# Places for other steps among the scans of a vision network: products at a unit's end, readings at the next one's beginning

## The chip, the cores and the metric

The kernel runs on one core of a Trainium2 chip. A core has five engines, each with its own queue of instructions that it takes strictly in order: TensorE (PE, matrix products, which reach their readers only through the small memory PSUM), VectorE (DVE), ScalarE (ACT), GpSimd (POOL), and SyncE (SP), which issues most transfers. Engines wait for one another by semaphores. The metric is the device time of one execution in microseconds (us); less is better.

## The reference

A two-layer network on four images of 256 channels and 32x32 pixels (1024 pixels an image), all in float32. Layer 0 (an attention with a selection of scores, and a mixture of eight small experts) is not touched by the change. Layer 1 is

```python
x = x + L1_conv(ln_c(x))                    # selective scan in four directions
t = tokens(x); x = x + L1_ffn(ln_t(t))      # two of eight experts for each token
```

with the two parts cut to what matters:

```python
def _selective_scan(x, A_log, D, W_delta, b_delta, W_B, W_C):
    delta = softplus(x @ W_delta + b_delta)
    Bm, Cm = x @ W_B, x @ W_C               # 16 states
    dA = exp(delta[..., None] * -exp(A_log))
    dBx = (delta * x)[..., None] * Bm[:, :, None, :]
    h = scan of  h = dA * h_before + dBx  over the 1024 pixels
    return einsum('bln,blcn->blc', Cm, h) + x * D
# the mean of four scans: forward, backward, rows from the last, columns from the last

def _L1_ffn(x, Wr, br, ln_g, ln_b, W1, b1, W2, b2):
    top_p, top_idx = top_k(softmax(x @ Wr + br), 2)
    xn = (x - mean) * rsqrt(var + 1e-5)
    y[e] = gelu((xn * ln_g[e] + ln_b[e]) @ W1[e] + b1[e]) @ W2[e] + b2[e]   # 256 -> 1024 -> 256
    return the two chosen y, weighted by top_p / sum(top_p)
```

## The kernel before, in words

**Scans.** An image is kept with channels on partitions, as two halves `c` of 128 channels. The kernel goes through 4 images x 2 halves x 16 states = 128 *units*, written out by hand under a manual schedule: the function `turn(k)` issues the instructions in the order in which each engine will take them. Per unit VectorE runs three scans of 128x1024: `forth` (L1505) over the pixels, `back` (L1514) over them backwards, and `columns` (L1531); and the small scan `come` (L1520). The third direction comes from the forward scan by a correction that GpSimd multiplies out (`third`, L1525). TensorE adds the four directions in PSUM by products with an identity matrix (`add`, L1500; `columns`, L1535), into two PSUM tiles `hp` per unit. VectorE multiplies them with C (`output`, `yc`, L1541), and TensorE sums the 16 states into `y` (L1542). After 16 states VectorE adds `y` to `x` (L1545). ScalarE makes the decays (`da_c` L1479, `prod` L1483, `da` L1487) and turns the inputs to columns (`uu` L1493), one unit ahead; GpSimd makes `uu` (L1492). At the first state of a half VectorE makes the running sum `cum` (L1571).

In `turn(k)` the order is: loads for unit k+2; `cum` and the column decays of k+1; `third` of k-1; products of k+1; `forth` and `back` of k; decays and inputs of k+1; `output` of k-1; `come_in` of k; then a place for *steps*; then `columns` of k.

**Steps.** Beside the scans other work goes in small pieces, written as generators that `yield` after each: `norm` (mean, transposes with the router's logits, variance, two reciprocal roots) and `route` (best two experts, ranks, slots) of the image whose scans have just ended, and `Prep.steps` of the next one: mean (`ln_mean` L1390), variance (`ln_var` L1399), scaling (`ln_rb`), B and C (`bp` L1426), and softplus in four blocks (`zp` L1438, ScalarE L1443 to L1449, VectorE L1447 to L1456, where `up` is L1447). The two are chained, first norm and route, then the preparation. Each unit takes one step, every fourth two, all in the place after `come_in`. A step often holds the reading of the previous step's product together with the next product. The steps' PSUM tiles share four buffers, tag `hp`, with the scans' own. After routing, `scatter` issues one indirect transfer a unit on GpSimd that puts tokens into their experts' slots.

**Experts.** The second stage goes over tiles of 256 tokens, each of one expert: `inputs` (transposes L1649, scaling to `xe` L1652, places of the results `to` L1655), `hidden` (L1664, Gelu on ScalarE L1666), `result` (L1672, `ys` L1675, and two indirect transfers L1677 on GpSimd to the rows that `to` names). 17 *early* tiles, of tokens of the first three images, run under a manual schedule with the steps of the last image's norm, route and scatter, one step after `hidden` and one after `result`. Then 19 *late* tiles follow. The tiles' buffers rotate in twos. A last stage adds each token's two results.

Of the kernel before, what the change touches and what calls it, by code (L numbers as in the profile page):

```python
# [11 lines left out]
F32 = mybir.dt.float32  # L12
F16 = mybir.dt.float16
BF16 = mybir.dt.bfloat16
I32 = mybir.dt.int32
# [6 lines left out]
P = 128  # L22
# [21 lines left out]
EARLY = (2 * (B - 1) * L - E * (T - 1) + T - 1) // T  # L44
W = C + 2
# [12 lines left out]
def metaformer(ctx: ExitStack, tc: tile.TileContext, t: dict, out: bass.AP):  # L58
# [1129 lines left out]
    def route(b, space, psum, tag):  # L1188

        used = 0  # L1190

        def room(shape):
            nonlocal used
            size = math.prod(shape)
            view = space[:, used : used + size]
            used += size
            return view if len(shape) == 1 else view.rearrange("p (a b) -> p a b", b=shape[1])
# [14 lines left out]
        best(m1, hot1)  # L1212
        nc.vector.tensor_scalar(tok[:, :, C + 1], red, -1.0, float(E), ALU.mult, ALU.add)
        nc.vector.tensor_copy(tok[:, :, C], goal[:, ts(b, NT)])
        yield
# [13 lines left out]
        nc.tensor.matmul(sums[:, 1].rearrange("p n e -> p (n e)"), mean_w, flat, start=True, stop=True)  # L1229
        nc.vector.tensor_scalar(m1, m2, 1.0, None, ALU.add)  # L1230
# [5 lines left out]
        place, pick, slotf = room([E, NT]), room([NT, E]), room([NT])  # L1236
        nc.vector.tensor_scalar(tote, sums[:, 1].rearrange("p n e -> p e n"), float(C), None, ALU.mult)
        nc.vector.tensor_copy(place, sums[:, 0].rearrange("p n e -> p e n"))
# [7 lines left out]
        yield  # L1246
        for k in range(2):
            nc.vector.tensor_tensor(pick, hots[k], place.rearrange("p e n -> p n e"), ALU.mult)
            nc.vector.tensor_reduce(slotf, pick, AX.X, ALU.add)
            nc.vector.tensor_copy(slot[:, k], slotf)  # L1250
        if b < B - 2:
            return
        yield
# [3 lines left out]
        if b == B - 2:  # L1257

            nc.vector.tensor_tensor(more, counts, limits, ALU.is_ge)
            nc.vector.tensor_reduce(tiles, more, AX.X, ALU.add)  # L1260
            ends = early.fill(room, tiles, done)
            nc.vector.tensor_tensor(left, tiles, ends, ALU.subtract)
            nc.vector.tensor_scalar(left, left, float(EARLY), 0.0, ALU.add, ALU.max)
            nc.vector.tensor_tensor(done[:, :E], left, tiles, ALU.min)
        else:

            nc.vector.tensor_scalar(count, count, float(T - 1), None, ALU.add)
            nc.vector.tensor_tensor(more, counts, limits, ALU.is_ge)
            nc.vector.tensor_reduce(tiles, more, AX.X, ALU.add)
            nc.vector.tensor_tensor(tiles, tiles, done[:, :E], ALU.subtract)  # L1270
            ends = late.fill(room, tiles, done)
            nc.vector.tensor_scalar(extra, ends[0:1, E - 1 : E], USUAL - EARLY + 0.5, None, ALU.is_gt)

# [9 lines left out]
    def norm(b, pool, psum, tag, raw_tag, d):  # L1283


        for h in range(NHALF):
            cols = ts(h, HALF)
            mean = psum.tile([P, HALF], F32, tag=tag, name="nm_mean")
            for c in range(CT):
                nc.tensor.matmul(mean, mean_w, x[b][:, c, cols], start=(c == 0), stop=(c == CT - 1))  # L1290
            yield
            for c in range(CT):
                nc.vector.tensor_tensor(d[:, c, cols], x[b][:, c, cols], mean, ALU.subtract)
        var = pool.tile([P, NT], F32, tag="nm_var", name="nm_var")
        raw = psum.tile([P, HALF], F32, tag=raw_tag, name="raw")[:, : NT * E].rearrange("p (n e) -> p n e", e=E)
        for r in range(NT // 2):
            tp = psum.tile([P, 2, C], F32, tag=tag, name="nm_tp")
            for i in range(2):
                n = 2 * r + i
                for c in range(CT):  # L1300
                    nc.tensor.transpose(tp[:, i, ts(c, P)], d[:, c, ts(n, P)], ident)
                for c in range(CT):
                    nc.tensor.matmul(raw[:, n], d[:, c, ts(n, P)], rw1[:, c, :], start=(c == 0), stop=(c == CT - 1))
            yield
            nc.scalar.copy(tok[:, ts(r, 2), :C], tp)
            for i in range(2):
                n = 2 * r + i
                nc.scalar.activation(tp[:, i], tp[:, i], AF.Square, scale=C ** -0.5, accum_out=var[:, n : n + 1])
        yield
# [3 lines left out]
        def rsqrt(dst):  # L1313

            nc.scalar.activation(sd, ve, AF.Sqrt)
            yield
            nc.vector.reciprocal(r0, sd)
            nc.vector.tensor_tensor(sd, r0, r0, ALU.mult)
            nc.vector.tensor_tensor(sd, sd, ve, ALU.mult)
            nc.vector.tensor_scalar(sd, sd, -0.5, 1.5, ALU.mult, ALU.add)  # L1320
            nc.vector.tensor_tensor(dst, r0, sd, ALU.mult)


        nc.vector.tensor_scalar(ve, var, 1e-5, None, ALU.add)
# [4 lines left out]
        nc.vector.tensor_tensor(lg1, raw, s1.unsqueeze(2).to_broadcast([P, NT, E]), ALU.mult)  # L1329
# [7 lines left out]
    with ExitStack() as st:  # L1337
# [34 lines left out]
        class Prep:  # L1372
# [9 lines left out]
            def steps(self):  # L1382
# [12 lines left out]
                yield  # L1395
                var = ps_m.tile([P, HALF], F32, tag="hp", name="ln_var")[:, :NT]
                for n in range(NT):
                    for c in range(CT):
                        nc.tensor.matmul(var[:, n : n + 1], sq[:, c, ts(n, P)], mean_w[:, 0:1],  # L1399
                                         start=(c == 0), stop=(c == CT - 1))  # L1400
                yield
                ve, sd, r0, rr, rs = (p1.tile([P, NT], F32, tag=f"ln_{i}", name=f"ln_{i}")
                                      for i in ("ve", "sd", "r0", "rr", "rs"))
                nc.vector.tensor_scalar(ve, var, 1e-6, None, ALU.add)
                nc.scalar.activation(sd, ve, AF.Sqrt)
                yield
# [4 lines left out]
                nc.vector.tensor_tensor(rs, r0, rr, ALU.mult)  # L1411
                for h in range(NHALF):
# [8 lines left out]
                yield  # L1421
                bc = p1.tile([P, 4 * HALF], F32, tag="sp", name="bc")[: 2 * NS, :L]
                for h in range(NHALF):
                    bp = ps_m.tile([P, HALF], F32, tag="hp", name="bp")[: 2 * NS]
                    for k in range(CT):
                        nc.tensor.matmul(bp, wbc[:, k, :], xm[:, k, ts(h, HALF)],  # L1426
                                         start=(k == 0), stop=(k == CT - 1))
                    nc.scalar.copy(bc[:, ts(h, HALF)], bp)
                nc.sync.dma_start(self.bc, bc)
                yield  # L1430


                for c in range(CT):
                    for h in range(NHALF):
                        cols = ts(h, HALF)
                        zp = ps_m.tile([P, HALF], F32, tag="hp", name="zp")
                        for k in range(CT):
                            nc.tensor.matmul(zp, wd[:, k, ts(c, P)], xm[:, k, cols],  # L1438
                                             start=(k == 0), stop=(k == CT - 1))
                        dd = self.delta[:, c, cols]  # L1440
# [4 lines left out]
                        nc.scalar.activation(v, v, AF.Exp, scale=-1.0)  # L1445
                        yield
# [4 lines left out]
                        yield  # L1451
                        nc.vector.tensor_tensor(v, v, ru, ALU.mult)
                        nc.vector.tensor_tensor(v, v, ln, ALU.add)
                        nc.vector.tensor_tensor(dd, dd, v, ALU.add)
                        nc.vector.tensor_tensor(self.dx[:, c, cols], dd, xm[:, c, cols], ALU.mult)  # L1455
                        nc.vector.scalar_tensor_tensor(x[b][:, c, cols], xm[:, c, cols], dsk[:, c : c + 1],  # L1456
                                                       x[b][:, c, cols], ALU.mult, ALU.add)
                    yield

        class Scan:  # L1460
# [51 lines left out]
            def back(self):  # L1512
                hs = p2.tile([P, L], F32, tag="h", name="h", bufs=4)
# [15 lines left out]
            def columns(self):  # L1529
                hs = p2.tile([P, L], F32, tag="h", name="h", bufs=4)  # L1530
# [20 lines left out]
        scans, steps, ys, cum = [], iter(()), [], None  # L1551
        sending = iter(())

        def routed(b):
            nonlocal sending
            yield from norm(b, p1, ps_m, "hp", "hp", p1.tile([P, CT, L], F32, tag="xm", name="nm_d"))
            yield from route(b, p1.tile([P, 4 * HALF], F32, tag="sp", name="numbers"), ps_m, "hp")
            sending = scatter(b)

        def turn(k):  # L1560
            nonlocal steps, cum
            if 0 <= k + 2 < len(order):
# [14 lines left out]
            if 0 <= k < len(order):  # L1577
                b, c, s = order[k]
                if c == 0 and s == 0:
                    for steps_left in (steps, sending):  # L1580
                        assert next(steps_left, "end") == "end"
                    steps = routed(b - 1) if b > 0 else iter(())
                    if b + 1 < B:
                        preps.append(Prep(b + 1))
                        steps = chain(steps, preps[-1].steps())
# [9 lines left out]
            if 0 <= k < len(order):  # L1595
                scans[k].come_in()
                for _ in range(1 + (s % 4 == 3)):
                    next(steps, None)
# [11 lines left out]
    with ExitStack() as st:  # L1610
# [3 lines left out]
        class Tile:  # L1614
# [28 lines left out]
            def inputs(self, ps_t):  # L1643
# [10 lines left out]
                self.to = pb.tile([P, T // P], I32, tag="to", name="to")  # L1654
# [13 lines left out]
            def result(self, ps_y):  # L1668
# [5 lines left out]
                ys = pb.tile([P, T // P, C], F32, tag="ys", name="ys")  # L1674
# [6 lines left out]
        with ExitStack() as sa:  # L1681
# [5 lines left out]
            with tc.manual_schedule():  # L1687
                todo = [Tile(early, i, "xa", EARLY) for i in range(EARLY)]
                for i in range(EARLY):
                    todo[i].slots()  # L1690
                    if i < 2:
                        todo[i].weights()
                b = B - 1
                steps = chain(norm(b, pa, psa, "t", "raw", pa.tile([P, CT, L], F32, tag="nm_d", name="nm_d")),
                              route(b, pa.tile([P, 4 * HALF], F32, tag="sp", name="numbers"), psa, "t"), scatter(b))
                next(steps)
                todo[0].inputs(ps_t)
                for i in range(EARLY):
                    todo[i].hidden(ps_h)
                    next(steps, None)  # L1700
# [5 lines left out]
                    next(steps, None)  # L1706
                for _ in steps:
                    pass
# [112 lines left out]
```

## Time and profile before

| | us |
|---|---|
| median of 3 runs | 4604.15 (4597.9 to 4604.52) |
| the profiled execution | 4614.54 |
| its span, first to last instruction | 4612.8 |
| scans, 128 units (2553.78 to 3897.50) | 1343.7 |
| early experts (to 4255.16) | 357.7 |
| late experts (to 4562.95) | 307.8 |
| last stage | 49.9 |

The first 2553.8 us are layer 0 and the preparation of image 0. In the profile, a line of the timeline gives start, duration, engine, source line, operation, the tiles written and read, their shapes, and in brackets how long the engine had stood idle before it and what ended that. A line of the waits gives who waited, for whom, the total in us, how often, and the longest. Consecutive equal instructions are merged (x4); matmuls are pipelined, so a group's start-to-start distance says more than its duration. Units are counted from 0, and unit k starts at the k-th `forth` scan.

### The profile page before, as it was taken

To read this page: it belongs to the slowest core of one execution; us is meant where nothing else is said; L and a number is where in the kernel's file an instruction comes from. 1 tells how busy PE (TensorE), PEld (TensorE's weight loads), DVE (VectorE), ACT (ScalarE), POOL (GpSimd) and SP (SyncE) were. 2 spreads that over 40 slices of the span, in tenths; PEclk is the share of its full clock that TensorE was granted. 3 is DMA by queue.
4 is the path that set the end of the run, shared out by engine and by line. 5 is a ranking of instruction groups with operands and counts; after the bars stand their busy time and mean duration, and the time that the engine had idled before them with its cause. 6 is when DMAs were issued, how large, how long until landed. Compare 5 with 4: busy or idle time off the path is not lost. (4 is left out here: it accounts for less than half of the span.)

```text
span 4612.8 us, 51296 instructions
## 1 busy us (share of the span) xinstructions
PE 3950.6 (86%) x18522; PEld 2185.2 (47%) x18522; DVE 3048.3 (66%) x5101; ACT 2888.6 (63%) x3788; POOL 1630.3 (35%) x1257
## 2 busy tenths in 40 slices
PE   7478878888888887789999799999999999887996
PEld 5143434443444443466665334443443434666785
DVE  3788899898989898322223799878788797110112
ACT  3989999999899898221112677667667665221222
POOL 0255445554555454310000345345345454011110
PEclk9578877887787788879999899999999999899997
DMA  9200000000000000100000233233333334444555
GB/s 288 56 1 1 10 1 1 1 10 1 1 1 10 1 1 10 38 1 0 0 1 23 79 100 121 97 98 106 100 102 101 100 117 126 136 139 139 177 182 183
DMA packets 171771, 306.82 MB, mean 67 GB/s; under 512 B 27753, under 2 KB 116594, under 8 KB 171506
## 3 DMA queue, kind: packets, MB, share of 16 engines
q1 hardware_dynamic: 161184, 284.10, 19.8%
q0 software_dynamic: 6528, 17.90, 1.1%
q8 instruction: 150, 2.46, 0.2%
q10 hardware_dynamic: 3794, 1.42, 0.1%
q14 instruction: 115, 0.94, 0.1%
HBM read 246.68 MB, written 56.69 MB: 66 GB/s over the span
## 5 line engine op out<-in xcount | busy, mean ns | idle before, releaser
L542 POOL TENSOR_SCALAR dr<-s_n,last 128x1024 bf16<-128x1024 f32 x256 | 730.2, 2871 | 873.3 <-DVE state L570 386.4
L458 ACT ACTIVATE junk_a<-s_n,state 128x1024 int8<-128x1024 f32 x448 | 514.6, 1149 | 24.1 <-DVE state L576 7.6
L1525 POOL TENSOR_TENSOR da_c<-prod,come 128x1024 f32<-128x1024 f32 x128 | 257.6, 2012 | 673.7 <-DVE h L1531 620.9
L1666 ACT ACTIVATE hid<-hp,b 128x256 f32<-128x256 f32 x288 | 134.2, 474 | 472.8 <-PE hp L1664 443.1
L462 DVE TENSOR_SCALAR_CACHE_REDUCE junk_v<-s_n,state 128x1024 int8<-128x1024 f32 x320 | 408.6, 1277 | 8.8
L1664 PE MATMUL hp<-xe,w 128*128 128x256 f32 x1152 | 296.0, 408 | 66.5 <-ACT hid L1666 43.5
L509 DVE SCALAR_TENSOR_TENSOR w<-s_n,win 128x1024 f32<-128x1024 f32 x256 | 349.0, 1363 | 5.2
L1113 DVE SCALAR_TENSOR_TENSOR acc<-y,tk_comb,acc 128x256 f32<-128x256 f32 x256 | 120.9, 483 | 349.6 <-PE y L1111 345.7
L1535 PE MATMUL hp<-h,ident 128*128 128x512 f32 x512 | 272.2, 658 | 65.0 <-DVE h L1531 65.0
L512 DVE MAX8 win<-w 128x8 f32<-128x1024 f32 x256 | 314.5, 1228 | 8.8
L610 ACT ACTIVATE ex<-sT 128x1024 f32<-128x1024 f32 x256 | 247.0, 1015 | 114.3 <-PE sT L602 114.1
L1492 POOL TENSOR_TENSOR uu<-dx,bb 128x1024 f32<-128x1024 f32 x128 | 304.2, 2376 | 40.5 <-DVE dx L1455 40.4
L1106 ACT ACTIVATE hid<-hp,b 128x512 f32<-128x512 f32 x128 | 88.0, 688 | 345.7 <-PE hp L1104 344.9
L458 ACT ACTIVATE junk_a<-s_n,guess 128x1024 int8<-128x1024 f32 x256 | 294.1, 1149 | 7.4
L620 PE MATMUL o_ps<-ex,vT 128*32 128x256 f32 x2048 | 249.7, 460 | 50.6 <-ACT ex L610 40.6
L1505 DVE TENSOR_TENSOR_SCAN h<-da,uu 128x1024 f32<-128x1024 f32 x128 | 289.7, 2264 | 2.7 <-ACT da L1487 2.7
L1531 DVE TENSOR_TENSOR_SCAN h<-da_c,uu 128x1024 f32<-128x1024 f32 x128 | 291.1, 2274 | 0.1
L1514 DVE TENSOR_TENSOR_SCAN h<-da,uu 128x1024 f32<-128x1024 f32 x128 | 289.7, 2263 | 0.0
L1664 PEld LDWEIGHTS hp<-xe,w 128*128 128x128 f32 x1152 | 220.6, 201 | 135.7 <-ACT hid L1666 78.1
L1500 PE MATMUL hp<-h,twice 128*128 128x512 f32 x512 | 250.5, 610 | 39.2 <-DVE h L1505 25.6
L1483 ACT ACTIVATE prod<-cum,a_log 128x1024 f32<-128x1024 f32 x128 | 146.8, 1147 | 198.0 <-POOL da_c L1525 198.0
L1479 ACT ACTIVATE da_c<-delta,a_log 128x1024 f32<-128x1024 f32 x128 | 268.5, 2098 | 0.1
(516 smaller groups left out, 8155.5 us busy)
## 6 DMA issues: line engine op xcount, KB each, us to landing
bb<-bc_d SPq DMA_DIRECT2D x128, 512.0 KB, 5.0
cb<-bc_d SPq DMA_DIRECT2D x128, 512.0 KB, 4.2
w<-in_w SPq DMA_DIRECT2D x36, 1024.0 KB, 5.1
w2e<-in_w SPq DMA_DIRECT2D x36, 1024.0 KB, 5.5
slots_x<-zeros SPq DMA_DIRECT2D x1, 33282.0 KB, 127.4
y<-results SPq DMA_DIRECT2D x8, 1024.0 KB, 7.7
xs<-slots_x SPq DMA_DIRECT2D x19, 258.0 KB, 5.6
b2e<-in_b SPq DMA_DIRECT2D x36, 128.0 KB, 5.3
```

The lines of the kernel that those rows point to most:

```text
L458: nc.scalar.activation(junk, self.row(r), AF.Sign, bias=thr, scale=-1.0, accum_out=u)
L462: nc.vector.tensor_scalar(junk, self.row(r), thr, None, ALU.is_lt, ALU.add, accum_out=u)
L509: nc.vector.scalar_tensor_tensor(w, self.row(r), self.win[:, r, 0:1], self.row(r), ALU.is_gt if r < LAST_DVE else ALU.is_ge, ALU.subtract, ...
L512: nc.vector.max(out=self.win[:, r, 1:], in_=w)
L542: ins = nc.gpsimd.tensor_scalar(dr, self.row(r), self.last[:, r : r + 1], None, ALU.is_lt)
L1479: nc.scalar.activation(grid(self.da_c), cols_flipped(self.prep.delta[:, self.c]), AF.Exp, scale=self.decay)
L1492: nc.gpsimd.tensor_tensor(self.uu[:, 0], self.prep.dx[:, self.c], self.bb, ALU.mult)
L1505: nc.vector.tensor_tensor_scan(rows.rearrange("p r w -> p (r w)"), self.da, self.uu[:, 0], 0.0, ALU.mult, ALU.add)
L1514: nc.vector.tensor_tensor_scan(hs[:, ::-1], self.da[:, ::-1], self.uu[:, 0][:, ::-1], 0.0, ALU.mult, ALU.add)
L1531: nc.vector.tensor_tensor_scan(hs, self.da_c, self.uu[:, 1], 0.0, ALU.mult, ALU.add)
L1535: nc.tensor.matmul(cols_flipped(self.hp[h]), ident, grid(hs)[:, :, ts(h, half)], start=False, stop=False)
L1664: nc.tensor.matmul(hp[:, f % 2], self.w1[:, c, ts(f, P)], self.xe[:, c], start=(c == 0), stop=(c == CT - 1))
```

## The change

- Steps have two places in a unit: one at the beginning of `turn(k)`, ahead of everything, and the old one ahead of `columns`. In `norm`, `route` and `Prep.steps` a `yield` stands between every product of TensorE and what reads it, and empty places (two `yield`s in a row) are put where VectorE and ScalarE use each other's results, so that products always fall at a unit's end and readings at the next unit's beginning. Every fourth unit no longer takes a second step.
- `steps` is a list: the routing of the last image starts at an image's first unit, the next preparation at unit 7 (`BEHIND`; for image 0 at unit 0), and both go on side by side. The numbers of `route` have a tile of their own (`NUMBERS`), since `sp` is now in use at the same time.
- The logits `raw` take a PSUM tile per pair of token blocks, copied to `lg1` at once; before, one tile was held over all four pairs. The variance of a preparation is made in two halves. The last two VectorE operations of a softplus block (`rest`) go beside the next block.
- `h` of the scans has three buffers instead of four.
- Experts: `to` has eight buffers and `ys` four, instead of two each. In the early tiles each place takes two (finer) steps; when routing has ended, two scatters.

```diff
@@ norm
             for c in range(CT):
                 nc.vector.tensor_tensor(d[:, c, cols], x[b][:, c, cols], mean, ALU.subtract)
+            yield
...
-        raw = psum.tile([P, HALF], F32, tag=raw_tag, name="raw")[:, : NT * E].rearrange("p (n e) -> p n e", e=E)
         for r in range(NT // 2):
             tp = psum.tile([P, 2, C], F32, tag=tag, name="nm_tp")
+            raw = psum.tile([P, HALF], F32, tag=raw_tag, name="raw")[:, : 2 * E].rearrange("p (n e) -> p n e", e=E)
...
             yield
+            nc.vector.tensor_copy(lg1[:, ts(r, 2)], raw)
             nc.scalar.copy(tok[:, ts(r, 2), :C], tp)
...
@@ Prep.steps (rb, bp and softplus blocks; in short)
+                    yield
                     nc.scalar.copy(bc[:, ts(h, HALF)], bp)
-                nc.sync.dma_start(self.bc, bc)
-                yield
+                    if h == NHALF - 1:
+                        nc.sync.dma_start(self.bc, bc)
+                    yield
+                def rest(c, cols):
+                    nc.vector.tensor_tensor(self.dx[:, c, cols], self.delta[:, c, cols], xm[:, c, cols], ALU.mult)
+                    nc.vector.scalar_tensor_tensor(x[b][:, c, cols], xm[:, c, cols], dsk[:, c : c + 1],
+                                                   x[b][:, c, cols], ALU.mult, ALU.add)
...
                             nc.tensor.matmul(zp, wd[:, k, ts(c, P)], xm[:, k, cols],
                                              start=(k == 0), stop=(k == CT - 1))
+                        yield
...
                         nc.scalar.activation(v, v, AF.Exp, scale=-1.0)
+                        if last is not None:
+                            rest(*last)
+                        last = c, cols
+                        yield
                         yield
                         nc.vector.tensor_scalar(up, v, 1.0, None, ALU.add)
...
@@ Scan.back, Scan.columns
-                hs = p2.tile([P, L], F32, tag="h", name="h", bufs=4)
+                hs = p2.tile([P, L], F32, tag="h", name="h", bufs=3)
@@ turn
+            for step in steps:
+                next(step, None)
             if 0 <= k + 2 < len(order):
...
-                    steps = routed(b - 1) if b > 0 else iter(())
+                    steps = [routed(b - 1)] if b > 0 else []
                     if b + 1 < B:
                         preps.append(Prep(b + 1))
-                        steps = chain(steps, preps[-1].steps())
+                if b + 1 < B and c * NS + s == (BEHIND if b > 0 else 0):
+                    steps.append(preps[b + 1].steps())
...
                 scans[k].come_in()
-                for _ in range(1 + (s % 4 == 3)):
-                    next(steps, None)
+                for step in steps:
+                    next(step, None)
                 scans[k].columns()
@@ Tile
-                self.to = pb.tile([P, T // P], I32, tag="to", name="to")
+                self.to = pb.tile([P, T // P], I32, tag="to", name="to", bufs=8)
...
-                ys = pb.tile([P, T // P, C], F32, tag="ys", name="ys")
+                ys = pb.tile([P, T // P, C], F32, tag="ys", name="ys", bufs=4)
@@ early tiles
+                def beside():
+                    for _ in range(2):
+                        if next(routing, "end") == "end":
+                            next(sending, None)
...
                     todo[i].hidden(ps_h)
-                    next(steps, None)
+                    beside()
```

## The prediction

> **What bounds the kernel now.** I read the busy times of the page first, then busy times by stage, then the start times of the scans unit by unit, then the waits of VectorE and TensorE in the scans, then single units in the timeline. The page's busy line shows no engine full over the whole span:
>
> ```profile
> PE 3950.6 (86%) x18522; PEld 2185.2 (47%) x18522; DVE 3048.3 (66%) x5101; ACT 2888.6 (63%) x3788; POOL 1630.3 (35%) x1257
> ```
>
> The change touches only the scans and the expert stage behind them. The stages (four images of scans, early experts, late experts; columns: stretch, its length, then busy time of PE, PEld, DVE, ACT, POOL, granted clock, DMA):
>
> ```profile
> 2553.78:2875.09 321.31, 303.75 (x706) 132.26 (x707) 289.28 (x245) 232.84 (x174) 146.77 (x95) 0.96 0.31 102
> 2875.09:3230.59 355.50, 326.18 (x781) 142.97 (x780) 296.00 (x294) 239.99 (x201) 164.03 (x112) 0.95 0.32 101
> 3230.59:3585.60 355.01, 325.54 (x781) 143.19 (x780) 296.28 (x295) 239.93 (x201) 163.78 (x112) 0.95 0.33 101
> 3585.60:3897.50 311.90, 294.12 (x699) 128.80 (x698) 275.09 (x270) 205.88 (x159) 159.42 (x111) 0.98 0.35 109
> 3897.50:4255.16 357.66, 300.49 (x1234) 231.19 (x1232) 47.64 (x145) 80.67 (x172) 48.02 (x49) 0.92 0.42 137
> 4255.16:4562.95 307.79, 279.15 (x1293) 237.42 (x1292) 34.57 (x77) 69.69 (x152) 36.48 (x38) 0.97 0.53 171
> ```
>
> A unit without other steps (timeline, DVE then PE):
>
> ```profile
> 3794.55 2.26 DVE L1505 TENSOR_TENSOR_SCAN h<-da,uu 128x1024 f32<-128x1024 f32 x1
> 3796.73 2.26 DVE L1514 TENSOR_TENSOR_SCAN h<-da,uu 128x1024 f32<-128x1024 f32 x1
> 3799.35 0.69 DVE L1541 TENSOR_TENSOR yc<-hp,cb 128x512 f32<-128x512 f32 x1 [0.36 <-PE hp L1500]
> ...
> 3800.95 2.26 DVE L1531 TENSOR_TENSOR_SCAN h<-da_c,uu 128x1024 f32<-128x1024 f32 x1
> 3803.13 2.26 DVE L1505 TENSOR_TENSOR_SCAN h<-da,uu 128x1024 f32<-128x1024 f32 x1
> 3794.86 1.88 PE L1542 MATMUL y<-yc,ident 128*128 128x512 f32 x4
> 3796.57 1.88 PE L1535 MATMUL hp<-h,ident 128*128 128x512 f32 x4
> ```
>
> Here TensorE bounds: five groups of four matmuls, 1.72 us from start to start, make 8.58 us a unit, and VectorE waits only a little at yc. Where VectorE waits for nothing, a unit takes it 7.85 us (unit 95). 32 units would take 274.6 us; the images take 46.7, 80.9, 80.4 and 37.3 us more, 245.3 together. Some of that is TensorE's own work for the steps, most of it is waiting. Unit 83, of 21.04 us, is the worst:
>
> ```profile
> 3447.79 0.21 DVE L1520 TENSOR_TENSOR_SCAN come<-prod,gap 128x32 f32<-128x32 f32 x1
> 3456.00 0.43 DVE L1447 TENSOR_SCALAR sp<-sp 128x512 f32<-128x512 f32 x1 [8.00 <-ACT sp L1445]
> 3457.07 2.28 DVE L1531 TENSOR_TENSOR_SCAN h<-da_c,uu 128x1024 f32<-128x1024 f32 x1
> 3452.13 1.88 PE L1438 MATMUL zp<-xm,wd 128*128 128x512 f32 x4
> 3459.41 3.73 PE L1535 MATMUL hp<-h,ident 128*128 128x512 f32 x4 [5.41 <-DVE h L1531]
> ```
>
> Two steps stand in one place there: TensorE's product, ScalarE's reading of it and VectorE's use of that, all ahead of the unit's third scan. VectorE waits 8.00 us, the scan is late, TensorE then waits 5.41 us for the scan and runs its next group at half speed (3.73 for 1.88). The waits in the scans, in total:
>
> ```profile
> DVE yc L1541 <- PE hp L1500: 104.8, 146, 10.5
> DVE sp L1447 <- ACT sp L1445: 30.6, 4, 8.0
> PE hp L1535 <- DVE h L1531: 65.0, 31, 5.4
> ```
>
> **The change, part by part.** It moves every reading of a step behind the unit in which TensorE made it: TensorE's part stays where steps stood (ahead of its columns group), the reading comes ahead of the next unit's first scan. It runs the routing of one image beside the preparation of the next (from unit 7) in place of one behind the other, splits the raw logits and the variances into pieces with PSUM of their own, and takes the second step out of every fourth unit. The work itself hardly changes: each routed image gains four VectorE copies (128x16; some 0.2 us each by the 0.21 of the 128x64 copy), the variance adds one row of 0.15 us; table loads, DMAs and matmuls keep their number.
>
> Costs of the pieces, S on TensorE and X on VectorE (timeline): half a mean S 1.72 (3372.53 to 3374.24), X 1.18; a pair of transposes with logits S 1.20 (3264.61 to 3265.81), X 0.2; half a variance S 1.85 (32 matmuls took 3.69), X 0.15; half an rb S 0.89, X 1.18; half of bp S 1.72; zp S 1.72 with 4.7 us on VectorE; the rank sums S 0.39.
>
> What a reading at the front of a unit costs: VectorE reaches it while TensorE is still behind, ahead of the step. TensorE's third group ends at t=0; VectorE ends its third scan at 3.6, TensorE its step at 5.16+S. So VectorE will wait about 2.5 us there, with a slack of 8.58-7.85=0.73. This is the wait that the change adds; behind it stand both first scans, and TensorE needs them. From the end of a step to the end of the next: semaphore 0.2, X, two scans 4.36, semaphore 0.2, TensorE's back and y groups 3.44, next step S: 8.2+X+S. TensorE alone needs 8.58+S. So a step with its reading costs S+max(0, X-0.38): half a mean 2.52, half an rb 1.69, the others S. Readings that need no TensorE fill the 2.5 us of waiting.
> A zp takes three units: 3x7.85+4.7=28.3 on VectorE against 27.5 on TensorE and 25.74 free; taken as 2.8 over. Before it was 3.0 (units of 11.30 and 8.92).
>
> Images 1 and 2 each: routing 0.8 (half a mean; its S lies in TensorE's wait at the image's start) + 2.5 + 4x1.2 + 2.3 (sums, and their reading together with the reciprocals) = 10.4; preparation 2x2.52 + 2x1.85 + 2x1.69 + 2x1.72 + 4x2.8 = 26.8. The two changes of half-image stay: three units of 10.05, 7.86 and 13.19 us where hardly a step stood (110 to 112), 5.36 over 25.74, twice 10.7 (cum, and x waiting 4.12 us for y). Sum 47.9 against 80.9 and 80.4.
> Image 0: preparation 26.8 less 3.4 of the mean, which lies under the start; the start stays (unit 1, 18.75 us, 10.2 over: the last piece of the first preparation); changes of half 5.4+1.5. Sum 40.5 against 46.7.
> Image 3: routing 9.5; ranks and tile list have no wait to hide in, 9.4 us of small VectorE rows less slack 0.73 in six units, 5.0; changes 4.6+5.4. Sum 24.5 against 37.3.
> All: 160.8 against 245.3, a gain of 84.
>
> Half-speed groups: after 32 one-column matmuls a group took 3.44 us in place of 1.72 (start 3395.10). None would be the low end, one after each variance half and each second pair the high end, 12 times 1.72; I take 16 us, near the high end, as such matmuls are still there. Gain 68.
>
> ScalarE keeps pace: a zp's Relu, Abs, Exp take 2.0 us at a unit's front, then its four rows of 2.1+1.15+1.12+1.97 follow; 8.5 us in a unit of 10. In the unit of Ln and Exp two table loads of 1.283 us join, and the decays end some 2 us ahead of the scan that reads them. Here a rule speaks against the change: the Trainium skill, "ScalarE: Activation LUTs", section "What ACT_TABLE_LOAD costs", has a switch of tables at about 2.66 us with a drain. By the page those two us would be gone and each of 16 zp would lose some 0.5 us, an estimate of 8 us in all; the trace has the next activation 0.01 us behind the load, so the row decides, with no loss.
>
> Fewer buffers for h (4 to 3) cost nothing: back of one unit then waits for the columns group two units earlier, which VectorE's yc has already waited out.
>
> The experts: eight places for `to` end VectorE's waits for the result scatter, 148.5 us in 17 tiles. But the next row waited for TensorE anyway:
>
> ```profile
> 4408.60 0.22 DVE L1655 SCALAR_TENSOR_TENSOR to<-xs,late_expert 128x2 int32<-128x2 f32 x1 [12.72 <-DMA results<-ys,to]
> 4409.61 0.69 DVE L1675 TENSOR_TENSOR ys<-yp,b2e 128x512 f32<-128x512 f32 x1 [0.79 <-PE yp L1672]
> ```
>
> This is the tightest tile, 0.79 us to spare; gain 0, at most TensorE's idle 0.80 us a tile, 15 us in 19. In the early experts two steps now go into a place where each step has been cut in two, so norm and ranks fall where they fell (the second root still stalls tile 4 by 3.47 us): 0. Slot scatters go four a tile instead of two: on POOL a tile then takes 5.4 for its results and some 3.3 a scatter, about 19 us against 17.63 a tile, for four tiles. Results come up to 6 us later, behind buffers that are now four and eight: 0; the late experts start behind TensorE's last product, not behind the scatter, which ended 27 us before. Both ends for this stage: -15 to +8 (one more tile at half speed, as tile 4 with 25.85 for 17.63).
>
> Sum: 4614.5 of the profiled execution (span 4612.8, 1.7 around it) less 68 is 4546; that execution lay 10.4 over the median, so 4536 for the median.
>
> **The rivals.** (a) *Readings cost nothing beyond TensorE's work.* Then the excess is TensorE's extra work, 84 us (sum of S), and 49 of half-changes and start, less 8 that lies under them: 125 against 245, a gain of 120, 4484. For it: TensorE is the bound of the plain unit. Against it: X over 0.38 must go somewhere.
> (b) *Two sequences at once crowd VectorE and ScalarE.* In units 8 to 15 of images 1 and 2 roots, token scaling (eight rows of 0.41) and squares stand ahead of ScalarE's decays. If each of these units loses 1.5 us and each zp 1.5: 16x1.5+12x1.5, 42 us given back, 4578.
> (c) *The wait at the front ends on the other side: slower.* There are about 57 readings that wait for TensorE (12, 19, 19 and 7). If VectorE never regains its lead, each costs the whole 2.5 us of waiting on top: 142 us, 4678. It decides from 68/57=1.2 us per reading on. For it: VectorE's slack is only 0.73. Against it: 8.2+X is shorter than 8.58 but for the mean and rb, and before, units with a waiting reading also cost less than that (9.05 to 9.89).
> (d) *The steps don't move apart.* Against it: the built order shows each reading ahead of the next unit's first scan, so no weight.
>
> **How the numbers follow.** Forecast 0.66, (a) 0.06, (b) 0.17, (c) 0.11. The range 4494 to 4584 takes the forecast without half-speed groups and with some gain in the experts (84+16, 4504, and a part of (a)) up to (b). Runs of this kernel differ by 0.14%, so 0.2% is about what can be told. Nearly all of forecast, (a) and (b) is faster: 0.86; between them and (c) 0.04 the same; 0.10 slower.
>
> **What would show it.** Right: no VectorE wait of 8 us at `up`; images near 318, 324, 324 and 301 us with the half-speed groups; VectorE waiting some 2.5 us for ln_mean, ln_rb, nm_mean and raw; TensorE's 65.0 us of waits for the third scan fall to the half-changes, about 30; the experts within 10 us of 358 and 308. Wrong: TensorE waiting for the forth scan in most step units (c), or decays late, shown as forth waiting for da (b).

## The result and the profile after

| | before | after | forecast |
|---|---|---|---|
| median, us | 4602.48 (4597.90 to 4604.52, 4 runs) | 4606.26 (4599.22 to 4614.73, 4 runs) | 4536 (4494 to 4584) |
| ratio to before | 1 | 1.001 (0.9991 to 1.003) | 0.985 |
| profiled execution, its span | 4614.54, 4612.8 | 4608.16, 4606.1 | |
| the scans over 274.6 us an image, by image | 46.7, 80.9, 80.4, 37.3 | 61.0, 70.8, 69.5, 40.6 | 40.5, 47.9, 47.9, 24.5, and 16 in all |

No change that can be measured; the forecast was faster by 68 us, and its range did not hold the time. The page's busy line after:

```profile
PE 3933.2 (85%) x18522; PEld 2160.5 (47%) x18522; DVE 3137.6 (68%) x5121; ACT 2887.2 (63%) x3788; POOL 1632.1 (35%) x1257
```

Twenty instructions more on VectorE, and 89.3 us more of its busy time: that is the line that does not fit. The stages after, columns as in the prediction:

```profile
2556.84:2892.44 335.60, 306.40 (x706) 128.62 (x707) 310.20 (x247) 232.46 (x174) 147.13 (x95) 0.97 0.29 97
2892.44:3237.85 345.41, 320.56 (x781) 134.76 (x780) 322.71 (x300) 239.78 (x201) 166.50 (x112) 0.99 0.32 104
3237.85:3581.95 344.10, 317.76 (x781) 133.41 (x780) 322.68 (x300) 239.62 (x201) 166.22 (x112) 1.00 0.33 105
3581.95:3897.18 315.23, 294.76 (x699) 127.03 (x698) 286.16 (x274) 205.46 (x159) 157.78 (x111) 0.98 0.35 108
3897.18:4251.00 353.82, 295.59 (x1234) 227.82 (x1232) 48.36 (x149) 80.69 (x172) 48.12 (x49) 0.93 0.43 139
4251.00:4560.00 309.00, 278.93 (x1293) 237.23 (x1292) 35.29 (x77) 69.69 (x152) 37.64 (x40) 0.98 0.53 171
```

VectorE's busy time (third pair) grew in each of the four images, by 20.9, 26.7, 26.4 and 11.1 us. The scans as a whole fell only from 1343.7 to 1340.3. Yet the waits that were to go went (scans; VectorE's, then TensorE's):

```profile
DVE x L1580 <- PE y L1577: 29.2, 7, 4.5
DVE lg L1317 <- PE raw L1315: 20.9, 12, 1.8
DVE yc L1576 <- PE hp L1535: 19.4, 51, 2.4
DVE nm_d L1304 <- PE nm_mean L1301: 8.6, 3, 3.3
...
DVE sp L1487 <- ACT sp L1483: 2.0, 1, 2.0
```

```profile
PE hp L1535 <- DVE h L1540: 90.8, 52, 25.6
PE hp L1570 <- DVE h L1566: 14.6, 7, 3.6
```

The waits of 8 us ahead of the third scan are gone, VectorE's wait at yc fell from 104.8 to 19.4, TensorE's for the third scan (L1566 now) from 65.0 to 14.6. In their place TensorE waits for the *first* scan (L1540): 90.8 us, of which 25.6 at the start were there before. VectorE is late there without waiting for anybody, because some of its rows take longer than they did. Its groups in the scans, after (busy us, mean ns), and the same rows before (other line numbers):

```profile
L1488 DVE TENSOR_TENSOR sp<-sp 128x512 f32<-128x512 f32 x14 | 29.0, 2072 | 0.5
L1458 DVE SCALAR_TENSOR_TENSOR x<-xm,dskip,x 128x512 f32<-128x512 f32 x12 | 28.8, 2401 | 0.0
L1484 DVE SCALAR_TENSOR_TENSOR sp<-sp 128x512 f32<-128x512 f32 x13 | 28.1, 2160 | 0.4
...
L1333 DVE TENSOR_TENSOR nm_sd<-nm_sd,nm_ve 128x8 f32<-128x8 f32 x6 | 10.6, 1768 | 0.2
...
L1238 DVE TENSOR_SCALAR numbers<-numbers 128x8 f32<-128x8 f32 x3 | 3.4, 1125 | 0.0
...
L1208 DVE TENSOR_REDUCE numbers<-lg 128x8 f32<-128x64 f32 x6 | 1.3, 220 | 0.2
```

```profile
L1453 DVE TENSOR_TENSOR sp<-sp 128x512 f32<-128x512 f32 x14 | 9.9, 705 | 0.4
L1450 DVE SCALAR_TENSOR_TENSOR sp<-sp 128x512 f32<-128x512 f32 x13 | 9.0, 693 | 0.4
L1456 DVE SCALAR_TENSOR_TENSOR x<-xm,dskip,x 128x512 f32<-128x512 f32 x12 | 8.9, 745 | 0.0
```

Three rows of the softplus take three times as long, 85.9 us for 27.8, and a row of eight elements a partition takes 1.77 us. One unit of the timeline, VectorE, then GpSimd, shows when:

```profile
3470.51 2.26 DVE L1549 TENSOR_TENSOR_SCAN h<-da,uu 128x1024 f32<-128x1024 f32 x1
...
3474.00 2.26 DVE L1566 TENSOR_TENSOR_SCAN h<-da_c,uu 128x1024 f32<-128x1024 f32 x1
3476.18 0.66 DVE L1487 TENSOR_TENSOR sp<-sp 128x512 f32<-128x512 f32 x1
3476.88 2.29 DVE L1488 TENSOR_TENSOR sp<-sp 128x512 f32<-128x512 f32 x1
3479.20 0.69 DVE L1489 TENSOR_TENSOR delta<-delta,sp 128x512 f32<-128x512 f32 x1
3479.81 2.28 DVE L1540 TENSOR_TENSOR_SCAN h<-da,uu 128x1024 f32<-128x1024 f32 x1
...
3488.26 2.40 DVE L1458 SCALAR_TENSOR_TENSOR x<-xm,dskip,x 128x512 f32<-128x512 f32 x1
```

```profile
3470.90 2.36 POOL L1527 TENSOR_TENSOR uu<-dx,bb 128x1024 f32<-128x1024 f32 x1
...
3476.42 2.20 POOL L1560 TENSOR_TENSOR da_c<-prod,come 128x1024 f32<-128x1024 f32 x1 [1.99 <-DVE h L1566]
...
3487.92 2.20 POOL L1560 TENSOR_TENSOR da_c<-prod,come 128x1024 f32<-128x1024 f32 x1 [2.01 <-DVE h L1566]
```

GpSimd's multiplication of the third direction starts as soon as VectorE's third scan has ended, and that is exactly the new place at the beginning of a unit. The row at 3476.18 begins ahead of it; the next one (3476.88) ends at 3479.17, 0.55 us after GpSimd's 3478.62; the row at 3488.26 ends at 3490.66, 0.54 after GpSimd's 3490.12. The backward scan at 3470.51 runs beside another GpSimd multiplication (3470.90) at its usual 2.26; one of its operands, `da`, lies in PSUM. The 20 forward scans of this trace that begin while the multiplication of `da_c` runs, with the same operand in PSUM, take 2.26 to 2.28 us, as usual. So the suspicion is that a VectorE instruction with two operands in SBUF is shut out while GpSimd reads there. The Trainium skill, "SBUF — State Buffer", section "Who interferes with whom", has this rule: the second SBUF input of VectorE goes through a port that it shares with GpSimd, whoever comes first holds it for the whole instruction, and the other is stopped, not slowed. The rows above agree: what is left of a held row behind GpSimd's end, 0.55 us, is a little less than an undisturbed row of that size takes (0.69).

Added up over the groups of the scans: the three softplus rows cost 58.1 us more than before (85.9 for 27.8), and seven small rows of norm and routing 33.7 more than where they met no GpSimd (in the fifth experiment below): `nm_sd` 10.6 for 1.0, the first mask of the routing 10.0 for 1.3, `place` plus `cum` 5.8 for 0.7, the slots' conversion 5.4 for 1.0, the sum for the weights 3.4 for 0.4, and two more 3.6 for 0.7. That is 91.8 us of VectorE's time. Two of these seven read only one operand from SBUF: the conversion and the sum for the weights (L1238, 1.13 us for 0.14). So two operands there are enough for a row to be held, but not needed. The reductions from SBUF are not held: L1208 begins beside the multiplication in all six cases and takes 0.22 us.

### The profile page after: what moved, and what is told of

The parts are those of the page before. It is cut to its first block, busy times and chain, and to the rows that moved or that the text cites. A ratio compares the mean times of both kernels' runs of the same rounds, so it can differ in the third digit from the quotient of the medians.

```text
span 4606.1 us, 51252 instructions
## 1 busy us (share of the span) xinstructions
PE 3933.2 (85%) x18522; PEld 2160.5 (47%) x18522; DVE 3137.6 (68%) x5121; ACT 2887.2 (63%) x3788; POOL 1632.1 (35%) x1257
## 3 DMA queue, kind: packets, MB, share of 16 engines
q10 hardware_dynamic: 3794, 1.42, 0.1%
## 5 line engine op out<-in xcount | busy, mean ns | idle before, releaser
L1535 PE MATMUL hp<-h,twice 128*128 128x512 f32 x512 | 253.2, 618 | 91.0 <-DVE h L1540 90.8
L1527 POOL TENSOR_TENSOR uu<-dx,bb 128x1024 f32<-128x1024 f32 x128 | 304.2, 2377 | 40.5 <-DVE dx L1457 40.5
L1540 DVE TENSOR_TENSOR_SCAN h<-da,uu 128x1024 f32<-128x1024 f32 x128 | 291.2, 2275 | 2.7 <-ACT da L1522 2.7
L1566 DVE TENSOR_TENSOR_SCAN h<-da_c,uu 128x1024 f32<-128x1024 f32 x128 | 289.8, 2264 | 0.0
L1522 ACT ACTIVATE da<-delta,a_log 128x1024 f32<-128x1024 f32 x128 | 142.8, 1115 | 211.4 <-DVE h L1549 211.4
L1112 PE MATMUL y<-w,hid 128*128 128x256 f32 x1024 | 262.9, 394 | 0.0
```

Of the source, the lines that this page charges most:

```text
L1112: nc.tensor.matmul(y, hid[:, f, ts(i, P)], w2[:, e, f, :], start=(f == 0), stop=(f == CT - 1))
L1527: nc.gpsimd.tensor_tensor(self.uu[:, 0], self.prep.dx[:, self.c], self.bb, ALU.mult)
L1540: nc.vector.tensor_tensor_scan(rows.rearrange("p r w -> p (r w)"), self.da, self.uu[:, 0], 0.0, ALU.mult, ALU.add)
L1566: nc.vector.tensor_tensor_scan(hs, self.da_c, self.uu[:, 1], 0.0, ALU.mult, ALU.add)
```

## The experiments

The theory, as it was put ahead of the runs: rows with two SBUF operands at a unit's beginning are held by GpSimd's multiplication (named P in the expectations of experiments 1 to 4, H in the later ones). The rival W: the readings and waits at a unit's beginning cost the time, whichever rows stand there. K and S are rivals within the theory and come with experiments 5 and 7. The medians of the kernel before beside these runs were 4601.64 us (experiments 1 to 4) and 4599.58 (5 to 7).

**1. The softplus rows back to the unit's end.** One more `yield` ahead of them, one less behind:

```diff
                         nc.scalar.activation(v, v, AF.Exp, scale=-1.0)
+                        yield
                         if last is not None:
                             rest(*last)
...
                         nc.vector.tensor_tensor(dd, dd, v, ALU.add)
-                        yield
+                yield
                 yield
                 rest(*last)
```

> The changed kernel with one thing moved: the VectorE rows of the twelve softplus blocks beside the scans (rest, up, and the three sums) go from the front of a unit, where GpSimd multiplies da_c, to the end place, between come and columns. Readings that wait for TensorE stay at the front. Theory P (VectorE rows with two SBUF operands are held by GpSimd's multiplication): the three rows of 2.28 to 2.40 us fall to about 0.69 to 0.75, a block's three units fall from 32.8 to about 28.3, the kernel gains 12 x 4.5, some 50 us against the changed kernel (about 4555). Theory W (waiting for TensorE at the front is what ate the gain): none of these rows waits for TensorE, so nothing is gained (about 4606).

Measured: 4553.11 us (4550.18 to 4555.19), ratio 0.9891 (0.9875 to 0.9908). From the first `forth` scan to the last, the scans take 1276.7 us, after 1331.8: 55 us less, for the 58.1 that these rows had cost. Three units with a softplus block fell from 32.8 us (11.50+10.78+10.51) to 27.95 (8.92+9.91+9.12); the prediction had 28.3. Twelve readings of `zp` and their waits stand where they stood, so W falls for these rows.

**2. All readings behind `come_in`.** The whole first place moves to the unit's end, readings first, products behind them:

```diff
-            for step in steps:
-                next(step, None)
+            begun = list(steps)
...
+                for step in begun:
+                    next(step, None)
                 for step in steps:
                     next(step, None)
```

> The changed kernel with the first place for steps moved from the beginning of turn(k) to just behind come_in, ahead of the place for TensorE's products; so a product is still read one unit later, but by VectorE between come and columns. Theory P: all long VectorE rows fall to their usual size, VectorE's busy time in the scans from 1242 to about 1157 us, and the gain that was forecast appears: images near 318, 324, 324, 303, together about 1269 for 1340, the kernel near 4535. Theory W: the same direction, but smaller than softplus alone can explain under P, since readings that wait for TensorE are only some 57 and TensorE waits for forth fall (90.8 us to under 40) while VectorE's busy time stays near 1242.

Measured: 4567.94 us (4557.11 to 4573.86), ratio 0.9926 (0.9902 to 0.9949), a miss of some 33 us; the scans take 1294.2. Here the PSUM tiles of the steps stay occupied for most of a unit longer, and TensorE waits for them with the next scan's group, which no wait did after the change:

```profile
PE hp L1535 <- ACT sp L1474: 27.3, 10, 3.6
PE hp L1570 <- DVE h L1566: 20.0, 11, 4.9
PE hp L1535 <- ACT nm_tp L1321: 13.5, 6, 2.3
```

40.8 us of waiting for ScalarE to free PSUM; VectorE's wait at yc, 104.8 us before the change and 19.4 after it, is back at 107.0. VectorE's busy time in the scans fell from 1241.8 to 1154.6 us, as P had said; W had it stay near 1242. So the held rows are gone here, but the new waits leave only 37.6 us of gain in the scans, where the fifth experiment has 80.6: the place at the unit's beginning is good for what reads PSUM, and bad for the rows that GpSimd holds.

**3 and 4. Without GpSimd's multiplication**, in the changed kernel and in the kernel before:

```diff
-                nc.gpsimd.tensor_tensor(grid(self.da_c), self.prod[:, :HW, :],
-                                        self.come.unsqueeze(2).to_broadcast([P, HW, HW]), ALU.mult)
                 self.add(grid(self.da_c), last=True)
```

> The changed kernel without GpSimd's multiplication of da_c (the third direction is left out: TensorE adds da_c as it is). Readings stay at the front. Theory P: no VectorE row at the front is longer than 0.75 us, busy time of VectorE in the scans near 1157, scans near 1265, the kernel near 4530. Theory W: readings at the front still wait for TensorE, so the scans stay within 15 us of 1340.

> The kernel before without GpSimd's multiplication of da_c, the same part left out, as the control of the run above. Theory P: in the kernel before hardly a VectorE row meets it, so little changes: 0 to -15 us (TensorE's third group and ScalarE's products no longer wait for GpSimd). Theory W: the same.

Measured: 4557.36 us (4552.19 to 4562.53), ratio 0.9902 (0.988 to 0.9925), for the changed kernel, and 4635.15, ratio 1.0071 (1.0051 to 1.0091), for the one before. The whole times can't be compared: without the third direction the data are others, and more tiles of experts are used, 1248 matmuls of the experts' `hp` in place of 1152, so three more tiles, and the kernel before is some 33 us longer in total with scans of the same length. The scans by themselves: 1244.3 us for 1331.8 in the changed kernel, 87.5 less, and 1333.1 for 1335.2 in the kernel before, 2.1 less. The multiplication costs the changed kernel's scans 87.5 us and the earlier kernel's next to nothing, although neither has TensorE waiting for it long (7.2 and 2.6 us). Two of the rows in the changed kernel without the multiplication:

```profile
L1488 DVE TENSOR_TENSOR sp<-sp 128x512 f32<-128x512 f32 x14 | 9.9, 706 | 0.4
...
L1333 DVE TENSOR_TENSOR nm_sd<-nm_sd,nm_ve 128x8 f32<-128x8 f32 x6 | 1.0, 166 | 0.2
```

That GpSimd's multiplication holds these rows is thereby shown: the same rows in the same place, 0.71 for 2.07 us and 0.17 for 1.77. P had said about 1265 for these scans, counted with the last unit; in that measure they took 1252.8. W had them stay within 15 us of 1340, and falls.

**5. The other held rows at the unit's end too.** Beyond the first experiment, the chains behind the roots, the maxima, places, picks and the list of tiles move by half a unit; what reads PSUM stays in front:

```diff
-        def rsqrt(dst):
+        def rsqrt(dst, turns):
             nc.scalar.activation(sd, ve, AF.Sqrt)
-            yield
-            yield
+            for _ in range(turns):
+                yield
...
-        yield from rsqrt(s1)
+        yield from rsqrt(s1, 1)
...
-        yield from rsqrt(s2)
+        yield from rsqrt(s2, 2)
@@ route
         nc.vector.tensor_tensor(both, hot1, hot2, ALU.add)
         yield
+        yield
...
         nc.vector.tensor_copy(place, sums[:, 0].rearrange("p n e -> p e n"))
+        yield
         nc.vector.tensor_scalar(m1, m2, 1.0, None, ALU.add)
...
         nc.vector.memset(keep[:, :, 0:1], 0.0)
-        yield
-        yield
...
             nc.vector.tensor_tensor(done[:, :E], left, tiles, ALU.min)
             yield
-            yield
@@ Prep.steps
                 nc.scalar.activation(sd, ve, AF.Sqrt)
                 yield
-                yield
                 nc.vector.reciprocal(r0, sd)
...
                 nc.vector.tensor_tensor(rs, r0, rr, ALU.mult)
                 yield
+                yield
```

> Beyond the softplus rows of the first experiment, every other VectorE row of the other steps that reads two operands from SBUF (the reciprocal chains of both norms, the two maxima with their one-hot masks, the places and picks of the routing, the list of tiles) is moved from the beginning of a unit to its end, half a unit earlier or later; readings of PSUM stay at the beginning. Theory H (the rows at the beginning are held by GpSimd's multiplication): the scans fall below the first experiment's 1276.7 us by about what taking the multiplication away showed beyond it (images 318.2, 326.3, 324.9, 307.3 against 314.7, 318.7, 319.0, 291.8, so 33 us at most, some 20 of it here), to about 1255, and the time to about 4532. Rival K (only the two softplus rows and the two long ones after them were held long enough to matter, and what is left is the number of instructions): no change against the first experiment, 4553.

Measured: 4536.52 us (4517.41 to 4543.74, 5 runs), ratio 0.9872 (0.9855 to 0.9888): faster than both kernels. The first experiment's median was 4553.11, and its fastest run (4550.18) lies above the slowest here (the intervals of the two ratios overlap a little); the scans take 1251.2 us for 1276.7, where H had said about 1255. K falls. Its four images:

```profile
2550.57:2868.97 318.40, 300.16 (x706) 130.79 (x707) 289.68 (x246) 231.96 (x174) 146.43 (x95) 0.97 0.30 103
2868.97:3188.45 319.48, 311.97 (x781) 137.12 (x780) 294.17 (x299) 239.28 (x201) 164.19 (x112) 0.99 0.35 113
3188.45:3506.80 318.35, 310.71 (x781) 136.34 (x780) 294.01 (x300) 239.41 (x201) 163.99 (x112) 1.00 0.35 113
3506.80:3801.80 295.00, 281.68 (x679) 123.95 (x678) 266.77 (x269) 205.15 (x159) 157.15 (x109) 0.99 0.35 115
```

VectorE's busy time in an image is back at 294 from 323, and the length of the images follows it, 318 to 319 from 345. (The last line ends at the start of the last unit, 8.5 us ahead of where the stages above end.) Of TensorE's waits for the first scan 9.1 us are left beside the start's 25.6; those for the third scan have grown from 14.6 to 25.1:

```profile
PE hp L1535 <- DVE h L1540: 34.7, 12, 25.6
PE hp L1570 <- DVE h L1566: 25.1, 19, 4.9
```

**6. The experts' buffers back at two.**

```diff
-                self.to = pb.tile([P, T // P], I32, tag="to", name="to", bufs=8)
+                self.to = pb.tile([P, T // P], I32, tag="to", name="to")
...
-                ys = pb.tile([P, T // P, C], F32, tag="ys", name="ys", bufs=4)
+                ys = pb.tile([P, T // P, C], F32, tag="ys", name="ys")
```

> The changed kernel with the experts' places and results back at two buffers each, the scans as changed. If the buffers are worth nothing, as forecast: 4606 within 9, the experts' stage within 5 us of 709. If they gave the 6.4 us by which that stage was shorter than before (708.9 against 715.3): about 4612, with the stage at 715.

Measured: 4604.54 us (4596.17 to 4622.53, 10 runs), ratio 1.0013 (1.0 to 1.0027), where the changed kernel has 1.001. Behind the scans it takes 708.0 us (3897.7 to 4605.7), the changed kernel 708.9, the one before 715.3. The buffers are worth nothing, and the 6.4 us by which that stage was shorter do not come from the buffers; whether those 6.4 us come from the finer steps of the early tiles or from the spread of one execution was not tried.

**7. GpSimd's multiplication in two halves.** How the two engines share: by bytes, or by whole instructions?

```diff
-                nc.gpsimd.tensor_tensor(grid(self.da_c), self.prod[:, :HW, :],
-                                        self.come.unsqueeze(2).to_broadcast([P, HW, HW]), ALU.mult)
+                for rows in (slice(0, HW // 2), slice(HW // 2, HW)):
+                    nc.gpsimd.tensor_tensor(grid(self.da_c)[:, rows], self.prod[:, rows, :],
+                                            self.come[:, rows].unsqueeze(2).to_broadcast([P, HW // 2, HW]), ALU.mult)
```

> The changed kernel with GpSimd's multiplication by the incoming states cut in two instructions of 128x512. Theory H (a row with two SBUF operands is kept out until the GpSimd instruction that runs has ended, and then goes first): the held rows of the softplus fall from 2.28 to about 1.0 + 0.66 = 1.7 us, some 0.6 us for each of about 100 held rows, and the scans by 30 to 50 us, less what a second instruction and a later third result cost; time about 4570. Rival S (both engines share what the memory gives, by bytes): the same bytes move in the same time, the held rows stay at 2.28 and the time at 4606 or a little above. A third way: GpSimd's second half goes ahead of the waiting row, which also leaves 2.28; then the row's start and end against the two halves tells it from S.

Measured: 4577.06 us (4566.37 to 4581.98), ratio 0.9949 (0.9929 to 0.9968); the scans 1300.6, 31.2 less than after the change. VectorE's groups in this kernel:

```profile
L1488 DVE TENSOR_TENSOR sp<-sp 128x512 f32<-128x512 f32 x14 | 18.6, 1331 | 0.4
L1458 DVE SCALAR_TENSOR_TENSOR x<-xm,dskip,x 128x512 f32<-128x512 f32 x12 | 18.4, 1533 | 0.0
L1489 DVE TENSOR_TENSOR delta<-delta,sp 128x512 f32<-128x512 f32 x14 | 18.4, 1314 | 0.4
L1484 DVE SCALAR_TENSOR_TENSOR sp<-sp 128x512 f32<-128x512 f32 x14 | 17.7, 1263 | 0.5
```

The means of the held groups, 2.07 to 2.40 us after the change, fell to between 1.26 and 1.53, so S, which has the same bytes in the same time, falls, and so does the third way, in which GpSimd's second half goes ahead. But L1489, free before at 0.69, is now held as well, 1.31: the two engines take turns by whole instructions, the waiting row behind the first half, the second half behind that row, the next row behind the second half.

```profile
3457.09 1.42 DVE L1488 TENSOR_TENSOR sp<-sp 128x512 f32<-128x512 f32 x1
3458.55 1.42 DVE L1489 TENSOR_TENSOR delta<-delta,sp 128x512 f32<-128x512 f32 x1
```

```profile
3456.63 2.79 POOL L1561 TENSOR_TENSOR da_c<-prod,come 128x512 f32<-128x512 f32 x2 [1.99 <-DVE h L1567]
```

Where three such rows stand in a row, halving gains almost nothing: from the first row's start to the last one's end 3.58 us (3456.39 to 3459.97) for 3.71 (3476.18 to 3479.89). Where one stands alone (L1458) it gains 0.87. That is why the gain lies at the lower end of what was expected.

## Why the prediction was wrong

- **What bounds, and where the waits are**: right. The excess over 274.6 us an image was mostly waiting, and the waits that were to go went: none of 8 us, yc from 104.8 to 19.4, the third scan from 65.0 to 14.6 (about 30 was forecast). VectorE's new waits for what TensorE had made were smaller than the some 2.5 us that were forecast for each: 1.7 us on the mean for `raw`, and with all other readings 42 us in 23 places (47 in 31 in the fifth experiment).
- **The step that failed: "A zp takes three units: 3x7.85+4.7=28.3 on VectorE".** The 4.7 us are rows timed at the unit's *end*, where GpSimd was idle or issued a transfer, and were used for the unit's *beginning*, where it multiplies. The block takes 32.8 there, 7.05 over 25.74 in place of 2.8; over 12 blocks 51 us. The same holds for "9.4 us of small VectorE rows less slack" in the routing and for the reciprocals of both norms: 33.7 us of holding. The scans gained 3.4 us in place of the 84 of the sum ahead of its half-speed term; the 91.8 us of held rows are of the size of the 80.6 between them, and without the multiplication 87.5 come back. The order of the work at the front was read from VectorE, ScalarE and TensorE alone; GpSimd's row there was not in the sum.
- **The profile of before could have shown it.** VectorE and GpSimd at the start of the scans, where both happened to meet:

```profile
2545.67 2.28 DVE L1571 TENSOR_TENSOR_SCAN cum<-inner,delta 128x1024 f32<-128x1024 f32 x1
2545.84 4.26 POOL L1492 TENSOR_TENSOR uu<-dx,bb 128x1024 f32<-128x1024 f32 x1 [40.39 <-DVE dx L1455]
2548.30 2.08 DVE L1447 TENSOR_SCALAR sp<-sp 128x512 f32<-128x512 f32 x1 [0.35 <-ACT sp L1445]
2550.41 0.69 DVE L1450 SCALAR_TENSOR_TENSOR sp<-sp 128x512 f32<-128x512 f32 x1
```

  A `tensor_scalar` of usually 0.42 us, with one operand in SBUF, took 2.08 beside a GpSimd multiplication that took 4.26 for its usual 2.36, having begun behind the scan `cum`, both of whose operands lie in SBUF. Inside the scans of that kernel, seven of GpSimd's multiplications of `da_c` took 3.73 us on the mean for 1.91, each begun behind a scan `cum`.
- **"What a reading at the front costs", S+max(0, X-0.38)**: right for readings of PSUM, as far as the fifth experiment shows it. With the held rows out of the way its images stand, in the measure of the first table, at 43.8, 44.9, 43.7 and 28.9 over (the last with 8.5 added for the last unit), 161.3 in all; the forecast's terms without the half-speed groups gave 40.5, 47.9, 47.9 and 24.5, 160.8. The agreement is of sums; single images are off by up to 4.4. Unit by unit the formula comes near as well: in image 1 half a mean takes 11.18 us (8.58+2.52=11.10 by the formula), a pair of transposes 9.87 (9.78), half of bp 10.06 (10.30). Units that hold other rows too are further off: 12.23 at the first half of the preparation's mean (11.10), 11.23 at the first half of an rb (10.27).
- **Half-speed groups, 16 us**: not settled. The scans of the fifth experiment come to 161 without this term, but slow matmuls are still in its trace: 29 of the some 2040 matmuls that fill the scans' `hp` took over 0.8 us for the usual 0.59, by an estimate from the 0.43 us between two starts some 12 us. So other terms were too large by about as much, or these fell into time that was lost anyway. They are fewer than before: TensorE's groups have a mean of 592 to 618 ns a matmul after the change, where the one behind the third scan had 659 before, and the granted clock is 0.97 to 1.00 for 0.95 to 0.98.
- **The experts, 0**: right (experiment 6).
- **ScalarE's tables, no loss**: nothing speaks against it; the first scan waits for its decays once in the whole of the scans, 2.7 us.
- **The rivals.** (b) had the size nearest to what happened, 42 us given back for 80.6, but not the cause: ScalarE's decays were not late. (c) was named with the sign that did show, TensorE waiting for the first scan, 52 times; its cause, a lead of VectorE that the new wait eats up, does not hold, as in the fifth experiment, with the held rows elsewhere and the readings where they were, TensorE waits 9.1 us. None of the rivals had VectorE's rows themselves become longer.

What stays open: the scans of the fifth experiment are 84 us shorter than before in the profiled executions, its median only 63 us. One execution of each kernel is profiled; that of before lay 12.1 us above the median of the table, that of the fifth experiment 19.1 below its own. In which part the executions of one kernel differ can't be read from one profile each. That the fifth experiment's median, 4536.52 us, is the 4536 of the forecast is chance: it is another order of the steps, and its scans gained 84 us in the profiled execution where the forecast had 68.

## What to carry to other kernels

The duration of an instruction belongs to its place and not to the instruction alone: before moving a row, look at what *every* engine does at the new place, the idle-looking ones too, and take its price from a row with the same neighbours. If an engine's busy time grows while the number of its instructions hardly does, compare mean durations by group before looking for waits; a held row shows as busy, and no list of waits has it. Here the rule that came out is simple: readings of PSUM go beside GpSimd's multiplication; rows with two SBUF operands, and the `tensor_scalar` and conversions that were held with one, go where GpSimd is idle. That alone turned no gain into 1.3%.

## What was not expected of the hardware

A row of 128x8 is held as long as one of 128x512: `nm_sd` took 1.77 us on the mean for 0.17, and the softplus row at 3476.88 took 2.29 for 0.69, both 1.60 us more. So small rows in a bad place cost ten times their length. VectorE and GpSimd take turns by whole instructions, so cutting one engine's instruction in two lets the other in between, and shuts it out again at the next (1.42 and 1.42 us for 2.29 and 0.69). And the hold works both ways: GpSimd's multiplication at 3476.42 took 2.20 us behind a VectorE row with two SBUF operands that had begun 0.24 us earlier, for 1.91 behind a scan with one of them in PSUM (the fifth experiment, at 3405.27) and 3.73 behind the scan `cum`.
